# The transformed 3x3 products in pieces of 64 moving columns instead of 128

## The chip, the cores and the metric

The kernel runs on one core of one Trainium2 chip. The time is that of the device, in microseconds (us), from the start of an execution to its end. A core has TensorE (PE in the profile; its weight loads are PEld), VectorE (DVE), ScalarE (ACT), GpSimd (POOL) and SyncE (SP), which here issues nearly all DMAs. Each engine works through its own instructions in order and waits for others by semaphores.

## The reference

The input x is 8 images of 512 channels with 32 x 32 points, all in float32. Two layers follow each other, each of the form x = x + f(groupnorm(x)) with groups of 16 channels.

The first layer is a chain of convolutions with two attention blocks in it:

```
t  = silu(bn(conv1x1(x)))             # 512 -> 512 channels
ys = [t[:, :256], t[:, 256:]]
for i in range(2):
    yi = ys[-1]
    z = silu(bn(conv3x3(yi)))         # 256 -> 256 channels: the products of this change
    z = attention(z)                  # 4 heads of 64, over all 1024 points
    z = silu(bn(conv1x1(z)))
    ys.append(yi + z)
out = silu(bn(conv1x1(concat(ys))))   # 1024 -> 512 channels
```

The second layer is a depthwise 3x3 convolution, batch norm, ReLU and a pruning of weak channels, then a 1x1 convolution of 512 to 512 channels with the same ending.

## The kernel before

Channels lie on the 128 partitions, points along the free dimension. The eight images go one after the other, and inside an image the two layers' blocks. Weights that don't stay on chip come through a ring of five tiles of 1 MB (`ring_load`, line 413), which SyncE fills from memory in the order in which they are used.

The 3x3 convolution is `conv3(l)` (line 725). It doesn't multiply by nine shifted images. Along the rows a transform of six taps for four results is used, across the rows one of four for two. The input `yp` holds the image in four column phases. `along_rows` and `across_rows` combine its phases on VectorE and write the transformed input to three tiles, `comps = kr, vt, qy`: one for each pair j of row taps, j = 0, 1, 2. Each tile holds four components c of 512 columns. The 512 columns are 2 (which row tap of the pair, i) x 2 (the half k of the 256 input channels) x 128 points. These three tiles are keys, values and queries of the attention later, so their names appear in the profile at the products: `ps_c<-kr`, `ps_c<-vt`, `ps_c<-qy`.

The transformed weights of one j and one half m of the output channels are one tile of the ring, `u[:, i, c, k, :]`, with 2 x 4 x 2 blocks of 128 x 128. `products(j, m)` (line 791) goes over c in the order 1, 2, 0, 3, over i, and over k. Each matmul multiplies one block of weights, as the stationary operand, by 128 columns of a component, the moving operand; the two values of k add up in PSUM. So 16 matmuls with 16 different blocks fill one PSUM tile of two banks, `ps_c3` (shown as `ps_c`), and then the next ring tile is requested. In the profile one float32 matmul of the program is two matmul records and two weight-load records.

`rows_back` (line 810) reads the PSUM tile: ScalarE copies the component c = 1 out (the row `c<-ps_c`), and VectorE makes two rows of results from the four components with four additions of 128 x 256. `along_back` and `ends` combine the three j, and `close` applies batch norm and SiLU and writes `z`, from which queries, keys and values (`ps_qk`, `ps_v`) are computed.

The order of all work is written out by hand in four strings, FIRST, HEAD, TAIL and LAST (lines 45 to 94). Each word in them is one piece of one stage: `P` is a call of `products`, `Rc` the copy, `R` the four additions, `d` a piece of the input transform, `B`, `E` and `Ez` the ends, `k`, `q` and `v` the products for keys, queries and values, `y` products of the first 1x1 convolution, `O` those of the last one of the image before. A stretch reads like this:

```
d ya P Rc R d*2 P Rc R d ya P d Rc R B P Rc R P B*2 Rc R E P Ez Rc B R E Ez y k*3 ya
```

The class `InOrder` (line 95) keeps every engine to the order in which its instructions are written; it is also why nearly all instructions carry line 105. PSUM gives the products two tiles of two banks (`big_tile`), which attention scores, value products and other stages share; three single banks and one small bank are the rest.

Of the kernel before, what the change touches and what calls it, by code (L numbers as in the profile page):

```python
# [15 lines left out]
P = 128  # L16
# [4 lines left out]
HEADS, HD = 4, 64  # L21
# [104 lines left out]
def fast_kernel(  # L126
# [16 lines left out]
    nc = Engines(tc)  # L143
# [18 lines left out]
    def big_tile(name):  # L162
        return ps_big.tile([P, 2, 512], F32, tag="big", name=name)
# [121 lines left out]
    def flat(ps):  # L285
        return ps.rearrange("p n f -> p (n f)")
# [126 lines left out]
    def ring_load(n=1):  # L413
        for _ in range(n):
            if not sources:
                continue
            if holds and len(sources) <= holds[0]:
                waiting[0] += 1
                continue
            src = sources.pop(0)  # L420
            t = ringp.tile([P, 2048], F32, tag="ring", name="wring")
            o = t[:, : src[1]]
            if src[1] == 1024:
                o = o.rearrange("p (k o) -> p k o", o=P)
            nc.sync.dma_start(o, src[0])
            ring.append(t)
# [298 lines left out]
    def conv3(l):  # L725
# [17 lines left out]
        def component(j, c):  # L743
            return comps[j][:, c * 512 : (c + 1) * 512]
# [46 lines left out]
        def products(j, m):  # L791

            ps = banks[j, m] = big_tile("ps_c3")
            u = ring.pop(0).rearrange("p (i c k o) -> p i c k o", i=2, c=4, k=2)
            for c in (1, 2, 0, 3):
                for i in range(2):
                    at = place[c] * 256 + i * P
                    for k in range(2):
                        nc.tensor.matmul(
                            flat(ps)[:, at : at + P],  # L800
                            u[:, i, c, k, :],
                            component(j, c)[:, (2 * i + k) * P : (2 * i + k + 1) * P],
                            start=(k == 0),
                            stop=(k == 1),
                        )
            ring_load()

        inner_planes, outer_planes, ys = {}, {}, {}
# [60 lines left out]
        for j in range(3):  # L869
            add("d", *[lambda j=j, i=i: along_rows(j, i) for i in range(2)])  # L870
            add("d", *[lambda j=j, i=i: across_rows(j, i) for i in range(2)])
        add("P", *[lambda j=j, m=m: products(j, m) for j, m in jm])
        add("Rc", *[lambda j=j, m=m: rows_back(j, m, 0) for j, m in jm])
        add("R", *[lambda j=j, m=m: rows_back(j, m, 1) for j, m in jm])
# [1000 lines left out]
```

## Time and profile before

| | |
|---|---|
| median of 2 runs | 2595.19 us (2595.06 to 2595.32) |
| span of the profiled execution | 2593.6 us |
| instructions | 36377 |
| TensorE matmuls busy | 2557.7 us (99%), 14806 records |
| TensorE weight loads busy | 1292.0 us (50%), 14806 records |
| VectorE busy | 2054.9 us (79%), 2954 instructions |
| ScalarE busy | 1214.4 us (47%), 1551 instructions |
| granted TensorE clock, mean | 0.997 |
| matmul records of ps_c | 3 x 1024, 128 x 128 stationary, 128 moving columns |

The profiled execution has a span of its own, 2593.6 us, 1.6 us under the median of the runs. In the profile's lines, a group of instructions is written as output <- inputs, with partitions x elements, the count, the busy time and the mean length of one; behind it stands the idle time of the engine just before. Matmul records overlap each other, and their ends are modelled, so that lengths of single records are longer than their spacing. "PE MATMUL" rows give the moving size, "PEld LDWEIGHTS" rows the stationary one; the tile of the array stands ahead of it, such as 128*128.

### The profile page before, as it was taken

How to read it: one execution, taken by the hardware profiler on the slowest of the kernel's cores; microseconds unless marked ns; L12 is line 12 of the kernel's file. 1: busy time of each engine (PE TensorE's matmuls, PEld its weight loads, DVE VectorE, ACT ScalarE, POOL GpSimd, SP SyncE). 2: the span in 40 equal slices, each digit the busy share in tenths (PEclk: the TensorE clock that was granted, in tenths of full speed). 3: DMA queues.
4: the chain of work that ended last, by engine and by line, in shares of the span. 5: the costliest groups of instructions: out<-in, count | busy, mean ns of one | idle time of the engine just before them, and what ended most of it. 6: DMA issues, size and time to landing. Idle time of an engine off the chain costs nothing.

```text
span 2593.6 us, 36377 instructions
## 1 busy us (share of the span) xinstructions
PE 2557.7 (99%) x14806; PEld 1292.0 (50%) x14806; DVE 2054.9 (79%) x2954; ACT 1214.4 (47%) x1551; POOL 129.2 (5%) x99
## 2 busy tenths in 40 slices
PE   8999999999999999999999999999999999999997
PEld 5454463634636346463464635545355544645443
DVE  8887588877897877877778778787788877888657
ACT  3635446353463544635445444544445454363534
POOL 1000000000100000000000000000001000010000
PEclk9999999999999999999999999999999999999998
DMA  9445230522305214060140702306122151312300
GB/s 347 157 155 203 66 122 25 167 98 73 113 27 199 66 65 122 17 247 18 65 122 17 248 18 81 105 24 241 33 96 75 61 204 34 130 45 82 122 17 34
DMA packets 83791, 268.51 MB, mean 104 GB/s; under 512 B 7072, under 2 KB 37536, under 8 KB 69408
## 3 DMA queue, kind: packets, MB, share of 16 engines
q1 hardware_dynamic: 76032, 248.01, 27.2%
q0 software_dynamic: 4032, 14.68, 3.1%
q10 hardware_dynamic: 3552, 3.41, 0.4%
q8 instruction: 118, 1.93, 0.3%
q14 instruction: 57, 0.47, 0.1%
HBM read 212.34 MB, written 36.96 MB: 96 GB/s over the span
## 4 chain that ended last, share of the span: by engine, by line
PE 95%; DVE 3%; ACT 1%; issue 0%; DMA 0%; SPq 0%; DVEq 0%; ACTq 0%
PE ps_av L105 16%; PE ps_s L105 16%; PE ps_c L105 13%; PE ps_cv L105 12%; PE ps_qk L105 8%; PE ps_cv2q L105 8%; PE ps_q L105 7%; PE ps_v L105 4%; PE ps_y L105 4%; PE ps_m L105 4%; PE ps_dn L105 1%; ACT qy L105 1%; DVE sum L105 1%; DVE ht L105 1%; PE ps_pw L105 0%
## 5 line engine op out<-in xcount | busy, mean ns | idle before, releaser
L105 ACT ACTIVATE e<-ps_s 128x1024 f32<-128x1024 f32 x512 | 509.7, 1023 | 286.8 <-PE ps_s L105 265.6
L105 PE MATMUL ps_s<-qy,kr 64*64 64x512 f32 x4096 | 513.7, 592 | 1.4
L105 DVE TENSOR_TENSOR sum<-sum,e 128x1024 f32<-128x1024 f32 x384 | 475.2, 1238 | 39.2 <-ACT e L105 19.9
L105 PE MATMUL ps_av<-e,vt 64*64 64x512 f32 x4096 | 506.2, 590 | 0.0
L105 DVE SCALAR_TENSOR_TENSOR ht<-xn,v_sb,ht 128x961 f32<-128x961 f32 (+1 forms) x256 | 317.3, 1247 | 8.6 <-ACT ht L105 5.0
L105 PEld LDWEIGHTS ps_s<-qy,kr 64*64 64x64 f32 x4096 | 160.5, 132 | 289.0 <-issue 191.1
L105 PEld LDWEIGHTS ps_av<-e,vt 64*64 64x64 f32 x4096 | 165.4, 133 | 277.4 <-issue 266.0
L105 PE MATMUL ps_qk<-z,wring 128*128 128x512 f32 x512 | 231.1, 596 | 2.0 <-ACT z L105 1.3
L105 DVE TENSOR_TENSOR sum<-e 128x1024 f32<-128x1024 f32 x64 | 78.1, 1220 | 164.0 <-ACT e L105 162.6
L105 ACT COPY c<-ps_c 128x256 f32<-128x256 f32 x96 | 35.6, 371 | 259.4 <-PE ps_c L105 259.3
L105 PEld LDWEIGHTS ps_qk<-z,wring 128*128 128x128 f32 x512 | 95.6, 190 | 115.7 <-issue 101.5
L105 DVE RECIPROCAL r<-ps_dn 128x128 f32<-128x128 f32 x128 | 113.7, 925 | 11.2 <-PE ps_dn L105 9.0
L105 PE MATMUL ps_c<-vt,wring 128*128 128x128 f32 x1024 | 119.4, 276 | 2.3 <-DVE v L105 1.3
L105 PEld LDWEIGHTS ps_c<-kr,wring 128*128 128x128 f32 x1024 | 116.8, 192 | 8.0 <-issue 6.1
L105 PEld LDWEIGHTS ps_c<-vt,wring 128*128 128x128 f32 x1024 | 116.2, 192 | 4.3 <-ACT c L105 2.3
L105 PE MATMUL ps_c<-qy,wring 128*128 128x128 f32 x1024 | 117.0, 275 | 0.0
L105 PE MATMUL ps_c<-kr,wring 128*128 128x128 f32 x1024 | 117.0, 275 | 0.0
L105 PE MATMUL ps_cv<-pt,w_sb 128*128 128x512 f32 x256 | 116.7, 607 | 0.0
L105 PE MATMUL ps_v<-wring,z 128*128 128x256 f32 x512 | 115.9, 379 | 0.7 <-DVE kr L105 0.7
L105 PEld LDWEIGHTS ps_c<-qy,wring 128*128 128x128 f32 x1024 | 115.6, 192 | 0.0
L105 PE MATMUL ps_m<-z,wm_sb 128*128 128x512 f32 x256 | 112.5, 592 | 0.0
L105 PE MATMUL ps_y<-pt,w_sb 128*128 128x512 f32 x256 | 112.3, 592 | 0.0
(178 smaller groups left out, 3255.5 us busy)
## 6 DMA issues: line engine op xcount, KB each, us to landing
wring<-u SPq DMA_DIRECT2D x96, 1024.0 KB, 4.8
pt<-in_x SPq DMA_DIRECT2D x32, 512.0 KB, 9.4
rw<-r SPq DMA_DIRECT2D x64, 256.0 KB, 3.4
xt<-in_x SPq DMA_DIRECT2D x32, 512.0 KB, 7.5
out<-xt SPq DMA_DIRECT2D x32, 512.0 KB, 8.0
kr<-r POOLq DMA_DIRECT2D x28, 512.0 KB, 6.6
wring<-q SPq DMA_DIRECT2D x14, 896.0 KB, 4.6
wring<-in_wqkv SPq DMA_DIRECT2D x16, 768.0 KB, 4.4
```

The lines of the kernel that those rows point to most:

```text
L105: made = method(*args, **kwargs)
```

## The change

Every matmul of `products` becomes two: the 128 moving columns are cut into two runs of 64 (the constant HD is 64), and each run is multiplied with both blocks of weights, k = 0 and k = 1, before the next run starts. The stationary operand stays 128 x 128 and is loaded once for each matmul. The block of weights used for one run is therefore loaded again for the other run. Results land in the same places of the same PSUM tile, the order of the components c and of i stays, and so do the readers, the ring and all other stages.

```diff
             for c in (1, 2, 0, 3):
                 for i in range(2):
                     at = place[c] * 256 + i * P
-                    for k in range(2):
-                        nc.tensor.matmul(
-                            flat(ps)[:, at : at + P],
-                            u[:, i, c, k, :],
-                            component(j, c)[:, (2 * i + k) * P : (2 * i + k + 1) * P],
-                            start=(k == 0),
-                            stop=(k == 1),
-                        )
+                    for n in (0, HD):
+                        for k in range(2):
+                            from_ = (2 * i + k) * P + n
+                            nc.tensor.matmul(
+                                flat(ps)[:, at + n : at + n + HD],
+                                u[:, i, c, k, :],
+                                component(j, c)[:, from_ : from_ + HD],
+                                start=(k == 0),
+                                stop=(k == 1),
+                            )
             ring_load()
```

## The prediction

> **What bounds the kernel now.** I read the page's busy line and chain first, then TensorE's timeline around the changed products, then the places where a weight load is not hidden.
>
> ```profile
> span 2593.6 us, 36377 instructions
> ...
> PE 2557.7 (99%) x14806; PEld 1292.0 (50%) x14806; DVE 2054.9 (79%) x2954; ACT 1214.4 (47%) x1551; POOL 129.2 (5%) x99
> ...
> PE 95%; DVE 3%; ACT 1%; issue 0%; DMA 0%; SPq 0%; DVEq 0%; ACTq 0%
> PE ps_av L105 16%; PE ps_s L105 16%; PE ps_c L105 13%; PE ps_cv L105 12%; PE ps_qk L105 8%; PE ps_cv2q L105 8%; PE ps_q L105 7%; PE ps_v L105 4%; PE ps_y L105 4%; PE ps_m L105 4%; PE ps_dn L105 1%; ACT qy L105 1%; DVE sum L105 1%; DVE ht L105 1%; PE ps_pw L105 0%
> ```
>
> TensorE's matmul stream sets the time: 95% of the chain, with no long gap. The changed products are the group ps_c, 13% of the chain. All time added to them lands on the path, less what waits around them can give back.
>
> ```profile
> L105 PE MATMUL ps_c<-vt,wring 128*128 128x128 f32 x1024 | 119.4, 276 | 2.3 <-DVE v L105 1.3
> L105 PEld LDWEIGHTS ps_c<-kr,wring 128*128 128x128 f32 x1024 | 116.8, 192 | 8.0 <-issue 6.1
> ```
>
> Each matmul of the program is two records, each with a load record of its own: 8 images x 2 layers x 3 planes x 2 output halves x 16 matmuls = 1536 matmuls, 3072 records in three groups of 1024. The means (276 and 192 ns) are lengths of pipelined records, not their spacing. Spacing I take from starts. First the chain around one layer's six products, in order of time (start, length, work):
>
> ```profile
> 969.70 10.30 PE ps_y L105 x24
> 980.00 21.44 PE ps_c L105 x192
> 1001.44 3.44 PE ps_y L105 x8
> ```
>
> 192 records in 21.44 us: **111.7 ns a record** at 128 moving columns. The other shapes have 24 ps_y records in 10.30 us (429 ns at 512 columns), and in the timeline 32 ps_v records between 1011.58 and 1018.48 us (215.6 ns at 256). From 256 to 512 columns that is (429.2 - 215.6)/256 = 0.834 ns a column and a fixed 2.1 ns. For 128 columns this line gives 108.9 ns, 2.8 less than seen: a first sign that at 128 columns something else has drawn level with the streaming.
>
> **What else costs.** The means of the group norm are products of 1 to 4 columns with a full 128-column load of their own, in the middle of the busy stream. First TensorE's rows, then the loads' rows of the same moment:
>
> ```profile
> 923.56 0.28 PE L105 MATMUL pm<-mv,g_sb 128*128 128x4 f32 x2
> 923.70 3.68 PE L105 MATMUL ps_cv2q<-z,wring 128*128 128x512 f32 x8
> ```
> ```profile
> 923.56 0.19 PEld L105 LDWEIGHTS pm<-mv,g_sb 128*128 128x128 f32 x1 [0.24 <-issue]
> 923.67 0.30 PEld L105 LDWEIGHTS ps_cv2q<-z,wring 128*128 128x128 f32 x2
> 924.22 0.19 PEld L105 LDWEIGHTS ps_cv2q<-z,wring 128*128 128x128 f32 x1 [0.24 <-issue]
> ```
>
> Loads start at 923.56, 923.67, 923.78 (two loads in 0.30 us, the last 0.19 long) and 924.22. While the moving side is 4 columns wide, loads follow each other every **0.11 us**; as soon as 512 columns stream, the next load waits 0.44. So a pair of load and matmul costs about 110 ns when almost nothing streams, and 111.7 ns when 128 columns do. A product of 64 columns lies between.
>
> Load records by width of the stationary operand (count; min/median/max ns):
>
> ```profile
> L105 PEld LDWEIGHTS pk<-ones,oks x2: 79/80/82, 2510.5 to 2510.5; 128*1 128x1 f32 x2
> L105 PEld LDWEIGHTS ps_dn<-sum,ones x256: 106/108/110, 121.6 to 2479.7; 128*32 128x32 f32 x128
> L105 PEld LDWEIGHTS ps_s<-qy,kr x4096: 129/133/133, 89.2 to 2476.1; 64*64 64x64 f32 x196
> ```
>
> With 192 at 128 columns: (192 - 80)/127 = 0.88 ns a column over a fixed part, 113 ns for the columns. Two readings of the load, spacing and slope, agree. It is not the rate of instructions: in attention, 64x64 loads come as four in 0.15 us, of which the last takes 0.13.
>
> **What the Trainium skill says.** "TensorE: Matmul & The Clock Gate", section "LDWEIGHTS (loading the stationary operand)": a load takes the stationary column count divided by 1.2, in ns, whatever the contraction depth; 106.7 for 128. The trace agrees (110 spacing). The section "Weight-path perf modes" of that page gives the fast weight load only to types other than FP32; all here is f32, and the 110 ns show no fast load. The section "Back-to-back issue gap" says that in a stream of load and matmul pairs both set the spacing; its 81 ns at 128 columns is not what this f32 trace has (111.7). "Perfetto Trace Analysis" says that TensorE's ends are a model: hence starts only.
>
> **The change, part by part.** (1) Each matmul becomes two with half the columns, each with its own load: 3072 records and 3072 loads of 128 columns are added; the stationary operands, sums and result places stay. Streaming per record falls to 64 x 0.834 + 2.1 = 55.5 ns, the load stays at 110. The longer one sets the spacing, as loads run one product ahead. (2) Spacing of the new record: between 110 (4 columns) and 111.7 (128 columns). I take 111.7, since at 128 columns the stream alone would need 108.9. Layer by layer: 384 x 111.7 = 42.9 us instead of 21.44. Sum: 3072 x 111.7 = 343 us; with 110, 338 us.
>
> (3) What the longer products give back. In these stages VectorE is almost as full as TensorE (us, PE, PEld, DVE, ACT busy, clock, DMA):
>
> ```profile
> 980.00:1001.40 21.40, 21.40 (x193) 21.40 (x193) 20.42 (x46) 3.73 (x11) 0.00 (x0) 1.00 0.61 212
> ```
>
> It transforms inputs and results of the same products, so where TensorE waits for it now, it won't. The first image's first layer takes from 43.73 to 67.49 us for 192 records, 2.3 more than 21.44. The second layers start at 479.21 and go on at 501.07, 21.86 instead of 21.44: 0.42 x 8 layers = 3.4 at most. The first image's second layer starts at 166.11 and ends near 188.9, 1.4 more than 21.44 (counted in part above). The waits of ps_qk and ps_v behind the last product in the first image (0.35 to 0.70 each in the timeline) go in part. Together about 7 us, at most 12. A check from the other side: TensorE is without work for 36 us in all (2593.6 - 2557.7); 11.6 of them lie ahead of the first convolution (8.26 + 1.42 + 1.09 + 0.84 in the timeline) and 16.7 in the last 65 us (48.27 busy), where nothing changes; 8 are left. (4) Weight ring: the same 1 MB per product from the same queue, now in twice the time; the DMA share of 0.61 falls to near 0.3, and transfers and input loads get slack. Cost nothing. (5) Readers: the copy of the second quarter and VectorE's four sums per product keep their places; with 7.1 us per product instead of 3.6 they wait more, which costs nothing as 20.4 us of VectorE lie beside 43. That idle time cannot be used elsewhere, since each engine's order is fixed. (6) The load queue: 64 pairs a product at the same spacing of pairs that the stage has today, so no faster supply of instructions is asked for.
>
> Sum: 343 - 7 = +336 on 2593.6, plus the 1.6 between the profiled span and the 2595.2 median of the runs shown: **2931 us**, 13% slower.
>
> **Rivals.** *Streaming sets the spacing after all* (load cheaper than it looks beside a running product): 6144 x 55.5 = 341 us against 343, or with the fixed part of the 128-column record (4.9 ns) 58.2 x 6144 = 358; 2593 to 2610 us, not slower. It decides the sign: the 2% (52 us), which is about what a measurement of this kernel tells from no change, is crossed at (343 + 52)/6144 = 64 ns a record. For it: the PE rows of the small product start only 0.07 us after each other. Against: its loads stand 0.11 apart and the following 512-column product pays the difference, its load coming 0.44 after the one before. Chance 4%; faster by over 2% would need under 47 ns, below the stream itself: 1%.
>
> *Load and stream don't overlap for short products*: 110 + 55 = 165 ns, 6144 x 165 = 1014, +671: 3260 us. Against: at 128 columns both are about 107 to 110 long and fit in 111.7 together. 3%.
>
> *The clock falls*, as the array streams in only half of these stages. The page shows 0.8 only in the last slice, with the wait at 2561 us. At the start the first 32 ps_cv records took 16.34 us where the next 32 of that shape took 13.90: 2.4 us is an estimate for one recovery. In 16 layers, some 40 us: 2970. 5%.
>
> *More is given back*: if the full 36 us of TensorE's idle time vanished, 2900. Against: where the idle time lies. 2%.
>
> **Range.** The main case has 85%; its own spread is load spacing 110 to 112 (338 to 344) and given back 2 to 12: 2920 to 2938. With a few us for the reading of 0.01 us stamps at the spacing (1 ns is 6 us over 6144 records), 2915 to 2945. The rivals left out hold 15%. Slower 95%, within 2% 4%, faster 1%.
>
> **What would show it.** ps_c records 6144, load records as many, 192 ns each as now; 384 records in about 42.9 us in the chain; busy share of VectorE in those stages near one half; other groups unchanged; chain share of ps_c up to about 23%. Loads spaced at 55 to 60 ns in these stages would prove me wrong, and so would a granted clock below 1.0 there, or 165 ns a pair.

## The result, and the profile after

The kernel with the change takes 2930.23 us (median of 2 runs, 2930.05 to 2930.40) against 2595.19 us before: 1.1292 times as long, 95% interval 1.1259 to 1.1324. The prediction said 2931 us, 13% slower.

The profile's page of the changed kernel, the lines that answer to those of before:

```profile
span 2928.3 us, 42504 instructions
...
PE 2895.0 (99%) x17878; PEld 1634.9 (56%) x17878; DVE 2062.4 (70%) x2954; ACT 1212.1 (41%) x1551; POOL 129.1 (4%) x99
...
PE ps_c L105 23%; PE ps_av L105 15%; PE ps_s L105 14%; PE ps_cv L105 11%; PE ps_qk L105 7%; PE ps_cv2q L105 7%; PE ps_q L105 6%; PE ps_v L105 4%; PE ps_y L105 4%; PE ps_m L105 4%; PE ps_dn L105 1%; ACT qy L105 1%; DVE ht L105 0%; PE ps_pw L
...
L105 ACT COPY c<-ps_c 128x256 f32<-128x256 f32 x96 | 35.7, 372 | 600.6 <-PE ps_c L105 600.6
...
L105 PEld LDWEIGHTS ps_c<-kr,wring 128*128 128x128 f32 x2048 | 231.1, 192 | 8.0 <-issue 6.3
L105 PE MATMUL ps_c<-vt,wring 128*128 128x64 f32 x2048 | 231.3, 275 | 0.0
```

There are 3072 matmul records more (17878 against 14806), all in ps_c, and as many loads. The mean record of 64 columns is 275 ns long, as that of 128 was (275 to 276): the record's length says nothing of the halved work, the spacing does. ScalarE's copy c now waits 600.6 us for ps_c, against 259.3; VectorE's and ScalarE's busy times are those of before within 0.4%, in a longer span.

The chain of the changed kernel around one layer's six products (start, length in us, work):

```profile
1093.50 10.30 PE ps_y L105 x24
1103.80 42.82 PE ps_c L105 x384
1146.63 3.49 PE ps_y L105 x8
```

384 records in 42.82 us is 111.5 ns a record, where 192 in 21.44 us were 111.7. The neighbours are unchanged at 10.30 and about 3.4 us. All sixteen stages of the chain are 42.81 to 43.07 us long, 685.4 us together; before, they lasted from 21.4 to 23.8 us each. And the busy time of one such stage (PE, PEld, DVE, ACT, then clock, DMA share, GB/s):

```profile
1103.80:1146.60 42.80, 42.80 (x386) 42.80 (x385) 21.40 (x47) 4.34 (x11) 0.00 (x0) 1.00 0.32 111
```

VectorE is busy half of it, DMA share has gone from 0.61 to 0.32, and the granted clock is still 1.00.

### The profile page after: what moved, and what is told of

The parts are those of the page before. It is cut to its first block, busy times and chain, and to the rows that moved or that the text cites. A ratio compares the mean times of both kernels' runs of the same rounds, so it can differ in the third digit from the quotient of the medians.

```text
span 2928.3 us, 42504 instructions
## 1 busy us (share of the span) xinstructions
PE 2895.0 (99%) x17878; PEld 1634.9 (56%) x17878; DVE 2062.4 (70%) x2954; ACT 1212.1 (41%) x1551; POOL 129.1 (4%) x99
## 3 DMA queue, kind: packets, MB, share of 16 engines
q8 instruction: 142, 2.33, 0.3%
## 4 chain that ended last, share of the span: by engine, by line
PE 97%; DVE 2%; ACT 1%; DMA 1%; issue 0%; SPq 0%; ACTq 0%; DVEq 0%
PE ps_c L105 23%; PE ps_av L105 15%; PE ps_s L105 14%; PE ps_cv L105 11%; PE ps_qk L105 7%; PE ps_cv2q L105 7%; PE ps_q L105 6%; PE ps_v L105 4%; PE ps_y L105 4%; PE ps_m L105 4%; PE ps_dn L105 1%; ACT qy L105 1%; DVE ht L105 0%; PE ps_pw L105 0%; DMA s<-scomb 0%; DVE xt L105 0%
## 5 line engine op out<-in xcount | busy, mean ns | idle before, releaser
L105 ACT COPY c<-ps_c 128x256 f32<-128x256 f32 x96 | 35.7, 372 | 600.6 <-PE ps_c L105 600.6
L105 DVE TENSOR_TENSOR mid<-ps_c,c 128x256 f32<-128x256 f32 x96 | 40.8, 425 | 330.5 <-ACT c L105 330.5
L105 PEld LDWEIGHTS ps_c<-kr,wring 128*128 128x128 f32 x2048 | 231.1, 192 | 8.0 <-issue 6.3
L105 PE MATMUL ps_c<-vt,wring 128*128 128x64 f32 x2048 | 231.3, 275 | 0.0
L105 PE MATMUL ps_c<-qy,wring 128*128 128x64 f32 x2048 | 231.3, 275 | 0.0
L105 PE MATMUL ps_c<-kr,wring 128*128 128x64 f32 x2048 | 230.5, 275 | 0.0
L105 PEld LDWEIGHTS ps_c<-qy,wring 128*128 128x128 f32 x2048 | 230.0, 192 | 0.0
L105 PEld LDWEIGHTS ps_c<-vt,wring 128*128 128x128 f32 x2048 | 230.0, 192 | 0.0
L105 PEld LDWEIGHTS ps_v<-wring,z 128*128 128x128 f32 x512 | 97.3, 190 | 28.0 <-issue 10.7
```

What stands on the lines that cost most here:

```text
L105: made = method(*args, **kwargs)
```

## The experiments

The theory: a load of 128 columns takes about 110 ns, runs beside the matmul before it, and sets the spacing of records once the moving side is shorter than that. Its rivals: the streaming sets it; load and stream add up; or every pair of load and matmul costs 111.5 ns by itself, whatever its shape. The last wasn't among the written rivals of the prediction, which set it aside on the ground that attention's four loads begin within 0.02 us.

**Four of 32 moving columns.**

```diff
-                    for n in (0, HD):
+                    for n in range(0, P, 32):
...
-                                flat(ps)[:, at + n : at + n + HD],
+                                flat(ps)[:, at + n : at + n + 32],
...
-                                component(j, c)[:, from_ : from_ + HD],
+                                component(j, c)[:, from_ : from_ + 32],
```

> Each product in four of 32 moving columns, each with its own load of 128 columns: 12288 records. Theory (the load of 128 columns sets the spacing, 111.5 ns whatever the moving width below 128): 12288 x 111.5 = 1370 us against 343, less the 8 us of waits that the first split gave back: 2593.6 + 1027 - 8 + 2 = 3614 us. Rival (streaming sets it, 0.834 ns a column and 2.1 ns fixed, 28.8 ns a record): 354 us, about 2605. Rival (load and stream of a short product don't overlap, seen already not to hold at 64): 138 ns a record, about 3950.

Measured: 4834.96 us, 1.863 times before: none of the three. The windows of its first stage (from 43 us on) show why; after each stretch and its length come PE, PEld, DVE, ACT, POOL, clock, DMA share, GB/s:

```profile
43.00:45.00 2.00, 2.00 (x20) 2.00 (x19) 1.97 (x4) 1.29 (x3) 0.00 (x0) 1.00 1.08 372
45.00:47.00 2.00, 2.00 (x20) 2.00 (x19) 1.97 (x4) 0.60 (x1) 0.00 (x0) 1.00 1.09 383
47.00:49.00 2.00, 2.00 (x12) 2.00 (x12) 0.17 (x1) 0.85 (x2) 0.00 (x0) 0.56 1.07 330
49.00:51.00 2.00, 2.00 (x11) 2.00 (x11) 0.00 (x0) 0.00 (x0) 0.00 (x0) 0.50 0.99 376
```

For some 4 us the loads start 111.5 ns apart (39 spacings between 42.89 and 47.24 us), just what the theory says. (The counts of a window, here 20 and 19, take in records that reach over its edges.) Then the granted clock falls to 0.50, although the records leave no gap, and the loads start 0.21 or 0.22 us apart. It stays so to the end of the stage. The chain of a later stage shows the whole of it, and what the next work pays:

```profile
1217.91 160.37 PE ps_c L105 x768
1378.27 5.35 PE ps_y L105 x8
```

768 records in 160.37 us are 208.8 ns each, the first few microseconds at full clock among them; at clock 0.50 alone the loads stand 213 ns apart (24 spacings between 1299.72 and 1304.84 us). The first eight of ps_y take 5.35 us instead of 3.49, until the clock is back. So the theory's spacing held while the clock did. A lower clock, to which the prediction had given 5% and 40 us for the change, came in this kernel, and cost some 1220 us against the 3614 of full clock.

**Three of 48, 48 and 32 columns**, to see where the clock falls.

```diff
-                    for n in (0, HD):
+                    for n, e in ((0, 48), (48, 96), (96, P)):
...
-                                flat(ps)[:, at + n : at + n + HD],
+                                flat(ps)[:, at + n : at + e],
...
-                                component(j, c)[:, from_ : from_ + HD],
+                                component(j, c)[:, from_ : from_ + e - n],
```

> Each product in three of 48, 48 and 32 moving columns, each with its own load: 9216 records. At full clock the load sets the spacing: 9216 x 111.5 = 1028 us against 343, less 8: 2593.6 + 685 - 8 + 2 = 3272 us. Streaming then fills 42.7 x 0.834 = 36 of 111.5 ns, 32%: between the two of 64 (48%, clock 1.00) and the four of 32 (24%, clock 0.50). If the granted clock falls here too, spacing is 208 ns as in the four of 32: 9216 x 208.5 = 1922 us, about 4190 us.

Measured: 4175.54 us, 1.608 times before: the second case. Two windows of its first stage:

```profile
44.00:54.00 10.00, 10.00 (x73) 9.76 (x72) 3.74 (x6) 2.35 (x3) 0.00 (x0) 0.82 1.04 374
54.00:64.00 10.00, 10.00 (x48) 10.00 (x49) 4.01 (x9) 0.61 (x3) 0.00 (x0) 0.50 0.59 222
```

At clock 0.50 the loads start 213 ns apart (47 spacings between 53.74 and 63.77 us), at a mean of 42.7 columns as at 32; the 208 ns expected were a stage's mean. With streaming in 32% of the time at full clock the clock falls, with 48% (the change) it does not. These shares are estimates, worked out from 0.834 ns a column and 111.5 ns a record.

**One of 96 and one of 32 columns.**

```diff
-                    for n in (0, HD):
+                    for n, e in ((0, 96), (96, P)):
...
-                                flat(ps)[:, at + n : at + n + HD],
+                                flat(ps)[:, at + n : at + e],
...
-                                component(j, c)[:, from_ : from_ + HD],
+                                component(j, c)[:, from_ : from_ + e - n],
```

> Each product in one of 96 and one of 32 moving columns instead of two of 64. Theory (load sets the spacing): 6144 records of 111.5 ns as with two of 64, 2930 us. Rival (load and stream of 64 add up partly, a sum or mix of both lengths): the mean length of stream is the same, so this gives no more than 2930 too, but the records of 96 and 32 would stand at different spacings; with the theory all stand at 111.5.

Measured: 2928.46 us (1.1285, 1.1264 to 1.1305), the same as with two of 64. One of its stages in the chain:

```profile
1102.85 42.80 PE ps_c L105 x384
```

All sixteen sum to 685.05 us for 6144 records, 111.5 ns in the mean; the granted clock is 0.998. Half of these records have 32 columns, as all have in the four of 32, and the clock holds: it is not the short matmul that brings it down. The single spacings also tell the theory from the rival: the loads from 1109.83 to 1111.84 us, which serve records of 96 and of 32 columns in turn, all start 0.11 or 0.12 us apart.

**The same weights twice in a row.** In the second run of 64 columns, k goes backwards:

```diff
-                        for k in range(2):
+                        for k in ((0, 1) if n == 0 else (1, 0)):
...
-                                start=(k == 0),
-                                stop=(k == 1),
+                                start=((k == 0) == (n == 0)),
+                                stop=((k == 1) == (n == 0)),
```

> The changed kernel with the order of k turned round in the second run of 64 columns (0, 1, then 1, 0), so that of every four matmuls the third has the same weights as the second. Theory (every matmul pays for its own load, the same weights or not): 2930 us. Rival (weights that are already there cost nothing again): 1536 of 6144 records at the 55.5 ns of their stream, 86 us less, 2844 us.

Measured: 2930.22 us (1.1292, 1.127 to 1.1315), with 685.49 us of ps_c in the chain against the change's 685.43. The program loads for each matmul, and a matmul whose weights were just used costs as much as any other. One limit: a float32 matmul is two records with a load each, and whether the last load of one and the first of the next hold the same part can't be read here.

**Stationary side cut too: 64 x 64 pieces.**

```diff
-                    for n in (0, HD):
-                        for k in range(2):
-                            from_ = (2 * i + k) * P + n
-                            nc.tensor.matmul(
-                                flat(ps)[:, at + n : at + n + HD],
-                                u[:, i, c, k, :],
-                                component(j, c)[:, from_ : from_ + HD],
-                                start=(k == 0),
-                                stop=(k == 1),
-                            )
+                    for h in (0, HD):
+                        for n in (0, HD):
+                            for k in range(2):
+                                from_ = (2 * i + k) * P + n
+                                nc.tensor.matmul(
+                                    flat(ps)[h : h + HD, at + n : at + n + HD],
+                                    u[:, i, c, k, h : h + HD],
+                                    component(j, c)[:, from_ : from_ + HD],
+                                    start=(k == 0),
+                                    stop=(k == 1),
+                                )
```

> As in the change, but each matmul cut once more, into two of 64 stationary columns (the halves of the output channels, to partitions 0-63 and 64-127 of the same PSUM tile): 12288 records of 64 x 64 columns, four in a row on one half. Theory (the load costs by its columns): a load of 64 takes half of 111.5, about 56 ns, as long as the stream of 64 columns; 12288 x 57 = 700 us against 343: about 2943 us, or less, down to before's 2595, where the two halves of the array run side by side. Rival (a pair of load and matmul costs 111.5 ns whatever its widths, a matter of the supply of instructions): 1370 us, about 3614.

Measured: 2698.81 us (1.04, 1.0381 to 1.0419). One stage in the chain, and its loads in the answer on the tile ps_c (count; min/median/max ns):

```profile
1020.06 27.93 PE ps_c L105 x768
```
```profile
L105 PEld LDWEIGHTS ps_c<-kr,wring x4096: 132/138/138, 43.7 to 2484.1; 128*64 128x64 f32 x196
```

Four times as many records as before, in 27.93 us: 36.4 ns a pair. A fixed cost of 111.5 ns for each pair is out, and with it the supply of instructions: twice the change's pairs go through in two thirds of its time. The load record is shorter with the stationary side (138 against 192 ns). The trace shows the loads of this stage starting 0.05 or 0.06 us apart, some of them two at nearly the same time (1030.11 and 1030.12 us). The first allows a load of 64 columns no more than the estimated 56 ns or so, which is also as long as its stream; the second, and a mean of 36.4 below it, says that the two halves of the array work side by side for part of the time. By this edit eight records in a row go to one half (two runs of columns, two k, two records each), not four as expected; that this order keeps the halves from overlapping more is likely, but no run tried another.

**Stationary side cut only**, on the kernel before: 64 stationary and 128 moving columns.

```diff
-                        nc.tensor.matmul(
-                            flat(ps)[:, at : at + P],
-                            u[:, i, c, k, :],
-                            component(j, c)[:, (2 * i + k) * P : (2 * i + k + 1) * P],
-                            start=(k == 0),
-                            stop=(k == 1),
-                        )
+                        for n in (0, HD):
+                            nc.tensor.matmul(
+                                flat(ps)[n : n + HD, at : at + P],
+                                u[:, i, c, k, n : n + HD],
+                                component(j, c)[:, (2 * i + k) * P : (2 * i + k + 1) * P],
+                                start=(k == 0),
+                                stop=(k == 1),
+                            )
```

> The kernel before, each product cut along the stationary side instead: two matmuls of 64 stationary and 128 moving columns, to partitions 0-63 and 64-127, so 6144 records. If the two halves of the array load and stream side by side, as the four 64 x 64 pieces of attention do: one stream of 128 columns for both, 108.9 to 111.7 ns per pair, 2586 to 2595 us. If they run one after the other, each is bound by its stream of 108.9 ns: 6144 x 108.9 = 669 against 343, about 2915 us.

Measured: 2593.99 us, 0.9996 times before (0.9987 to 1.0004): no difference. In the chain a stage of 384 records is:

```profile
981.30 21.11 PE ps_c L105 x384
```

110.0 ns for a pair of halves, against 111.7 for the whole. The two loads of a pair start within about 0.01 us of each other (984.89 and 984.90 us, for example), the next pair 0.11 us later: side by side. As many records and loads as the change has, and no cost: doubling the number of loads is not what hurts, loading 128 columns for 64 moving ones is. The stage's 0.33 us don't reach the time. Times 16 they would be 5 us, of which 1.2 were seen, and the interval takes in none at all. In the profiled run TensorE waits for weights in the ring, which the list of the kernel before doesn't have:

```profile
PE ps_c L105 <- DMA wring<-u: 3.9, 2, 2.5
```

These 3.9 us take up most of what the stages gained.

**VectorE's four sums per product done twice**, in both kernels. It shows whose time each stage is.

```diff
-            tt(even, ms[2], c1, ALU.add)
-            tt(odd, c1, ms[2], ALU.subtract)
-            tt(even, ms[0], even, ALU.add)
-            tt(odd, odd, ms[3], ALU.subtract)
+            for _ in range(2):
+                tt(even, ms[2], c1, ALU.add)
+                tt(odd, c1, ms[2], ALU.subtract)
+                tt(even, ms[0], even, ALU.add)
+                tt(odd, odd, ms[3], ALU.subtract)
```

On the kernel before:

> The kernel before with VectorE's four sums per product (rows_back) done twice. That is 4 x 0.34 = 1.36 us more of VectorE per product, 8.2 us per layer, 131 us in all. In the kernel before VectorE is busy 20.4 of a stage's 21.4 us, so some 7 us per layer come onto the path, less what the products behind the stage cover (3.4 us of ps_y): between 4 and 7.2 us x 16, 60 to 115 us more, 2655 to 2710 us. If VectorE had room there, 2595.

Measured: 2721.22 us (1.0486, 1.0469 to 1.0504), 127 us more, above the expected 60 to 115. Part of its chain in one stage; it now runs on VectorE:

```profile
1037.37 2.34 DVE qy L105 x4
1039.72 2.66 DVE mid L105 x8
...
1042.40 1.29 DVE sd L105 x2
1043.69 2.65 DVE mid L105 x8
1046.35 1.34 DVE y L105 x4
1047.69 1.20 DVE sd L105 x2
```

The 127 us have two parts. TensorE is without work for 129.7 us of this span (2718.8 less 2589.1 busy), against 35.9 before: 94 us more of waiting, within the expected range. So the kernel before had little room on VectorE in these stages. The other part is TensorE's busy time, 31 us longer for the same instructions. Some of it is the clock: after a wait of 3.0 us behind this stage it was granted 0.50 for some 7 us, and records of ps_qk started 0.85 instead of 0.43 us apart. The mean granted clock of this run is 0.991 against 0.997, which is about 16 us by estimate (0.006 x 2718.8); what the rest is was not traced.

On the changed kernel:

> The changed kernel with the same four sums done twice. Theory (in the changed stages VectorE has 20.4 us of work in 42.8, so it is half idle and the added 8.2 us lie beside TensorE): no cost but the last product's, at most 1.36 us per layer: 2930 to 2950 us. If VectorE still bounded the stage, 60 us and more, over 2990.

Measured: 2933.22 us (1.1303, 1.1284 to 1.1322), 3 us above the change. TensorE's waits in this kernel name the place:

```profile
PE ps_qk L105 <- DVE mid L105: 3.2, 2, 1.6
PE ps_v L105 <- DVE kr L105: 0.7, 2, 0.3
```

3.2 us in two waits, against 0.5 in the changed kernel. The same work that cost 127 us costs 3 beside the longer products.

## Why the prediction was right

**The spacing.** Step (2) took 111.7 ns for a record of 64 columns, from two places in the trace before: 110 ns where 4 columns stream, 111.7 where 128 do. Measured: 111.5. (Its other reading, 113 ns from the lengths of load records, rests on ends that are modelled; the runs test the spacing.) Of the rivals, streaming alone (55.5 ns) and the sum (165 ns) are excluded by the stages of the changed kernel itself. The four of 32 at full clock and the 96 and 32, both at 111.5 ns, show that the moving width below 128 doesn't matter while the clock holds; the 64 x 64 pieces and the stationary halves show that the load's width does.

**The count.** 3072 records more at 111.5 ns are 342.5 us; the span grew by 334.7.

**What was given back.** That leaves 7.8 us, where step (3) said 7, at most 12. Two waits of ps_c in the kernel before, 2.0 us together, are gone from the changed kernel's list:

```profile
PE ps_c L105 <- DVE v L105: 1.3, 1, 1.3
PE ps_c L105 <- ACT c L105: 0.7, 1, 0.7
```

The first image's first layer, 43.73 to 67.49 us before, is now 43.47 to 86.30, that is 42.83 long and without its 2.3 us of delay. Its second layer lost nearly all of its 1.4 (42.90 long now). The second layers of the other seven images, 0.42 over the first layers before, are as long as these now: 2.9 together. These three are some 6.5 of the 7.8. Not all waits went: the ps_qk of the first image still waits for VectorE, and ps_av has a new wait. TensorE's waits in the changed kernel:

```profile
PE ps_av L105 <- ACT part L105: 1.4, 1, 1.4
PE ps_v L105 <- DVE kr L105: 0.7, 2, 0.3
PE ps_qk L105 <- DVE mid L105: 0.5, 2, 0.3
```

The prediction's check from the other side, 8 us of idle TensorE left over, came to the same size by luck. TensorE's time without work fell by 2.6 us only, from 35.9 to 33.3 (2928.3 less 2895.0); the other 5.2 us of what came back lay where the busy figure counts work.

**Readers and ring, steps (4) and (5).** At no cost, as said: the DMA share went to 0.32 (0.3 was said), VectorE is busy 21.40 of 42.80, and the doubled sums, at 3 us, show that this idle time was real.

**The instructions, step (6).** Right, and shown by the 64 x 64 pieces; the fetch of instructions grew to 2.33 MB from 1.93 in the page's queues with no wait of TensorE for it.

**The clock.** The prediction gave a lower clock 5% and priced it at one recovery a layer, 40 us. It didn't fall in the changed kernel, so the forecast stands. The price was wrong, though: it left out that a fallen clock can stay down for the whole stage and that the loads slow down with it. In the three-piece kernel this costs 4175.54 against the estimated 3272 of full clock, some 900 us; in the changed kernel, by estimate, 6144 records at 213 instead of 111.5 ns would cost some 620. The change lies on the good side of that edge, at 48% of streaming where 32% falls off it. Neither the trace of before nor the prediction showed how near, and that the clock held was luck in so far as nothing in the prediction tells 48% from 32%.

## What to carry to other kernels

When a matmul stream is dense, ask for each shape which is longer, its stationary columns' load or its moving columns' stream, and read both from distances between starts; a tiny matmul in the middle of the stream (here the group norm's) gives the price of a load by itself. Here, cutting the moving side below that point bought nothing and paid a whole load for every piece, while a cut of the stationary side onto both halves of the array, at 128 moving columns, cost nothing. Look at the granted clock of every stage of such a kernel as well: two pieces cost what the loads cost, three and four also halved the clock. A stage in which an engine beside TensorE was nearly full hid little of that engine's further work; the same stage made longer hid nearly all of it.

## What the runs showed of the hardware that wasn't expected

The granted clock fell to 0.50 in stretches in which TensorE's records leave no gap, some 4 us into the first stage of the four of 32 columns. (The ends of these records are modelled, so they can't show whether the array itself stood still between short streams.) One difference between the kernels that fell and those that held is the streaming's share of the time: by estimate 24% and 32% fell, 48% (two of 64, or 96 and 32) held; where between 32% and 48% the edge is, and whether it is the streaming share or something that goes with it, wasn't tried. At clock 0.50 a load of 128 columns with its short matmul takes 213 ns instead of 111.5, 1.91 times as long. Two halves of the array take their loads side by side: 55.0 ns per record of 64 stationary and 128 moving columns (21.11 us for 384), 36.4 at 64 moving columns; what sets the 36.4 was not tried.
